# A two-layer RGCN with a GATv2 layer behind it: the RGCN layers staged a whole group apart, in half-group buffers

## The chip, the cores and the metric

The kernel runs on one core of a Trainium2 chip. The metric is the device time of one execution in microseconds, and for several executions their median. A core has five engines with a queue each: PE (TensorE, matmuls; its weight loads are listed apart as PEld), DVE (VectorE), ACT (ScalarE), POOL (GpSimd) and SP (SyncE, used here for DMA and for reading addresses). In this kernel POOL does little but issue the gathers.

## The reference

12,500 nodes with 128 features, 400,000 edges sorted by their target `dst`, 10 relations. The relation of an edge is the argmax of ten columns of its attributes.

```python
def _rgcn_layer(x, src, dst, edge_type, w_rel, root, bias):
    seg = dst * NUM_REL + edge_type
    sums = segment_sum(x[src], seg, num_segments=N * NUM_REL)
    cnt = segment_sum(ones(seg.shape), seg, num_segments=N * NUM_REL)
    mean = (sums / maximum(cnt, 1.0)[:, None]).reshape(N, NUM_REL, -1)
    return einsum('nrd,rdo->no', mean, w_rel) + x @ root + bias
...
h = relu(_layernorm(x))
h1 = relu(_rgcn_layer(h, src, dst, edge_type, w_rel1, root1, b1))
x = x + _rgcn_layer(h1, src, dst, edge_type, w_rel2, root2, b2)
h = relu(_layernorm(x))
# GATv2: 4 heads of 32, softmax over the edges of a target node
e = leaky_relu((h @ W_r)[dst] + (h @ W_l)[src], 0.2)
score = einsum('ehc,hc->eh', e, att)
x = x + segment_sum(softmax_by_dst(score) * (h @ W_l)[src], dst) + bias
```

## The kernel before

An RGCN layer is turned round: first every node's row is multiplied by all ten relation matrices, which makes a table of N x 10 rows in DRAM; then each edge fetches the row (source, relation), weighs it with 1/count, and the rows are summed by target node. `transform` makes the first table (98 tiles of 128 nodes: layer norm, transpose, three matmuls against `wall`, copies to SBUF, a DVE add of the bias, stores). `analyse` looks over the edges, and `sorted_edges` is the path that sorted edges take; the other path, `any_edges`, is not entered.

The 400,000 edges are 125 groups (G) of 128 x 25 (P x J): partition p holds 25 consecutive edges. Since targets are sorted, the nodes of a group lie in a window of 128 from a base node, and a sum by target is a matmul with a one-hot matrix. Three stages follow each other, each with a loop over the groups.

Layer 1 (`layer1`). `load` reads a group's attributes, finds the relation, makes the index `idx` (source x 10 + relation), issues 25 indirect DMAs on POOL (`gather`, L329; each fetches 128 rows of 512 bytes from the table) into one of three `xs` buffers, writes the wide one-hot `sb` in one DVE operation (L397) and counts edges by node and relation in 25 small matmuls (L401). `weights` completes the counts over the group's borders (three matmuls, L409 to L416), spreads them back to the edges through the one-hot `st` (L339, made in `by_node` from a broadcast of `drow_d`) in 25 matmuls (L422), and takes 1/count. `work` reads the base node (`base`: an ACT copy, L323, and a read on SP), and calls `sums`: 25 times a DVE one-hot scaled by the weight (`s`, L351, six buffers) and a matmul with it (L353), all into one PSUM tile. `carry` adds the border node's share from the group before (L359) and copies to SBUF (L362). Then come the own row, relu, a transpose (L128), three matmuls against `wall` (L445), ACT copies, and the stores of the second table. The loop calls `load(g)`, `weights(g-1)`, `work(g-2)`.

Layer 2 (`layer2`) gathers rows of the second table with the same `idx` and sums them with `sums` and `carry`; a layer norm, a transpose and one matmul make the tables of attention. Its loop calls `gather(g)` and `work(g-1)`.

Attention gathers rows of `h @ W_l` (132 wide), adds the target's row by matmuls (`pz`, L564 and L568), and makes scores (L571 to L574), maxima by scans, exponentials (`xw`, L626) and sums (L634). A group's `xw` is written after scores of the next two groups have been begun.

The framework sets each engine's order inside a stage by a planner with costs of its own, and adds the waits: a consumer waits for the notice (a semaphore count) of its producer, a writer of a buffer for the last reader of the buffer's older contents. In the program before, each matmul L353 waits for its one-hot and for its gather and gives a notice of its own.

## Time and profile before

| | |
|---|---|
| median of three runs | 15,672.79 us (15,643.28 to 15,676.48) |
| profiled execution, own time | 15,668.01 us |
| its span | 15,666.2 us |
| mean granted PE clock | 0.649 |
| busy share of the span | PE 47%, PEld 32%, DVE 38%, ACT 9%, POOL 62% |
| first gather of layer 1, of layer 2, of attention | 476.2, 5,650.7, 10,197.2 us |
| matmul instructions of L353 | 12,500 for 6,250 matmuls (two passes each) |

A row of the profile's groups names line, engine, operation, output and inputs, then its count, busy time and the mean in ns of one, and last how long the engine stood idle just before such instructions and what released it. "issue" as a releaser means that the profile shows nothing that the engine waited for; "remote" and "another core or an unknown queue" stand where no producer was found for the wait, though only one core runs. Idle time of an engine that is not the limit costs nothing, and so each stage has to be read by itself.

### The profile page before, as it was taken

The numbers are of one execution on the slowest core, as the hardware profiler recorded it, in microseconds if no ns is written. First come the engines' busy times: TensorE is split into PE (matmuls) and PEld (weight loads), VectorE is DVE, ScalarE is ACT, GpSimd is POOL, SyncE is SP. The second block draws the span as 40 slices with busy tenths as digits, with TensorE's granted clock in tenths as the row PEclk, the third lists the DMA queues.
The fourth block names the chain that finished last, engine by engine and source line by source line (L and its number), as shares of the span: only waits on it lengthen the run. The fifth ranks groups of instructions, "written<-read, shape, count | busy, mean of one in ns | idle before, by whom it ended". The sixth has DMA issues, their size and how long they took to land.

```text
span 15666.2 us, 128693 instructions
## 1 busy us (share of the span) xinstructions
PE 7415.8 (47%) x39724; PEld 5085.2 (32%) x39724; DVE 5907.1 (38%) x16500; ACT 1459.9 (9%) x4672; POOL 9747.0 (62%) x9384
## 2 busy tenths in 40 slices
PE   7344444444344433444344444445555555555555
PEld 2223333322232322333233333333333433333333
DVE  5333333333333322222222222244444544444444
ACT  2000000000000000000000000011111111111111
POOL 0566666666666656666666666656666666666665
PEclk9666666666666655555555555567766777767777
DMA  6322323323332211111111111122222222222221
GB/s 202 111 92 91 96 92 96 96 90 95 94 96 92 91 59 53 54 54 54 53 54 55 55 54 54 52 68 63 66 62 64 65 62 66 62 66 65 62 64 51
DMA packets 626065, 1164.38 MB, mean 74 GB/s; under 512 B 196480, under 2 KB 398830, under 8 KB 625390
## 3 DMA queue, kind: packets, MB, share of 16 engines
q0 software_dynamic: 300000, 621.40, 14.7%
q1 hardware_dynamic: 279544, 456.64, 8.8%
q10 hardware_dynamic: 45846, 78.02, 1.4%
q8 instruction: 341, 5.59, 0.1%
q14 instruction: 334, 2.74, 0.1%
HBM read 949.89 MB, written 205.49 MB: 74 GB/s over the span
## 4 chain that ended last, share of the span: by engine, by line
another core or an unknown queue 34%; POOL 19%; PE 19%; issue 14%; DVE 9%; DMA 4%; ACT 1%; ACTq 0%; SPq 0%; DVEq 0%; POOLq 0%
POOL xs L329 19%; PE ps L353 9%; DVE s L351 4%; PE pz L564 2%; PE pt L445 2%; DMA xs<-xl_d,src_i 2%; PE po L634 2%; DVE xw L626 1%; PE pz L568 1%; PE ps L150 1%; DMA xs<-t_d,idx 1%; DMA xt<-in_x_dram 1%; DVE sb L397 1%; PE ptr L128 1%
## 5 line engine op out<-in xcount | busy, mean ns | idle before, releaser
L329 POOL DMA_INDIRECT xs<-t_d,idx x6250 | 6310.8, 1010 | 3815.1 <-issue 2597.7
L353 PE MATMUL ps<-xs,s 128*128 128x128 f32 x12500 | 3119.0, 392 | 4870.9 <-issue 2743.4
L329 POOL DMA_INDIRECT xs<-xl_d,src_i x3125 | 3434.3, 1099 | 2014.9 <-DVE xw L626 1046.8
L353 PEld LDWEIGHTS ps<-xs,s 128*128 128x128 f32 x12500 | 2411.9, 267 | 5713.7 <-issue 3732.0
L351 DVE TENSOR_SCALAR s<-iota,dst_f,w 128x128 f32<-128x128 f32 x6250 | 2019.8, 359 | 5559.5 <-remote 3662.8
L564 PE MATMUL pz<-xs,ident 128*128 128x512 f32 x1750 | 1297.5, 834 | 2097.2 <-DMA xs<-xl_d,src_i 1219.8
L564 PEld LDWEIGHTS pz<-xs,ident 128*128 128x128 f32 x1750 | 355.6, 254 | 2229.6 <-issue 1559.7
L568 PEld LDWEIGHTS <-st 128*128 128x128 bf16 x9375 | 840.9, 126 | 622.7 <-issue 558.1
L572 DVE TENSOR_TENSOR lr<-lr,att 128x512 f32<-128x512 f32 x875 | 533.5, 624 | 1259.3 <-ACT lr L571 855.0
L568 PE MATMUL pz<-xr,st 128*128 128x128 bf16 x9375 | 956.5, 269 | 65.2 <-DVE st L339 49.9
L634 PE MATMUL po<-xw,s 128*128 128x132 f32 x6250 | 848.8, 297 | 76.5 <-DVE xw L626 41.2
L634 PEld LDWEIGHTS po<-xw,s 128*128 128x128 f32 x6250 | 815.9, 208 | 122.6 <-issue 64.4
L362 ACT COPY sm<-ps 128x128 f32<-128x128 f32 x250 | 66.3, 265 | 7564.5 <-PE ps L359 4030.8
L571 ACT ACTIVATE lr<-pz 128x512 f32<-128x512 f32 x875 | 476.8, 551 | 2776.4 <-remote 1425.1
L630 DVE TENSOR_TENSOR s<-iotab,dst_b 128x640 f32<-128x640 bf16 x625 | 506.6, 814 | 420.8 <-PE po L634 354.9
L626 DVE TENSOR_TENSOR xw<-xs,xw 128x640 f32<-128x640 f32 x625 | 484.0, 819 | 156.0 <-ACT xw L625 122.3
L574 DVE TENSOR_REDUCE sc<-lr 128x16 f32<-128x512 f32 x875 | 531.3, 620 | 1.0
L445 PE MATMUL pt<-wall,hT 128*128 128x512 f32 x750 | 504.3, 827 | 57.0 <-ACT hT L130 41.0
L397 DVE TENSOR_TENSOR sb<-iotab,dst_b 128x3200 bf16<-128x3200 bf16 x125 | 434.9, 3479 | 0.9 <-PE pcn L401 0.9
L424 DVE TENSOR_TENSOR cw<-pc,rh 128x250 f32<-128x250 f32 x125 | 51.9, 415 | 726.7 <-remote 619.8
L150 PE MATMUL ps<-wall,hT 128*128 128x512 f32 (+1 forms) x588 | 300.9, 647 | 29.1 <-DVE ts L155 21.4
L445 PEld LDWEIGHTS pt<-wall,hT 128*128 128x128 f32 x750 | 183.4, 268 | 305.1 <-issue 175.8
(187 smaller groups left out, 4532.6 us busy)
## 6 DMA issues: line engine op xcount, KB each, us to landing
db<-drow_d SPq DMA_DIRECT2D x250, 800.0 KB
xs<-t_d,idx POOLq DMA_INDIRECT x6250
t_d<-ts SPq DMA_DIRECT2D x125, 640.0 KB
m<-in_edge_attr_dram SPq DMA_DIRECT2D x125, 525.0 KB
t_d<-ts ACTq DMA_DIRECT2D x98, 640.0 KB
xs<-xl_d,src_i POOLq DMA_INDIRECT x3125
ac<-acc_d SPq DMA_DIRECT2D x250, 64.0 KB
xr_d<-xp SPq DMA_DIRECT2D x125, 96.0 KB
```

Source lines behind the costliest of these rows:

```text
L329: nc.gpsimd.indirect_dma_start(out=xs[:, j, :], out_offset=None, in_=table, in_offset=bass.IndirectOffsetOnAxis(ap=ids[:, j:j + 1], axis=0))
L351: nc.vector.tensor_scalar(s, iota, dst_f[:, g, j:j + 1], w[:, g, j:j + 1], op0=OP.is_equal, op1=OP.mult)
L353: nc.tensor.matmul(ps, s, xs[:, j, :], start=(j == 0), stop=(j == J - 1), skip_group_check=True)
L397: nc.vector.tensor_tensor(sb, iotab[:, None, :].to_broadcast([P, J, P]), dst_b[:, g, :, None].to_broadcast([P, J, P]), op=OP.is_equal)
L445: nc.tensor.matmul(pt[:, :n], hT, wall[:, c:c + n], start=True, stop=True)
L564: nc.tensor.matmul(pz[:, :n, :], ident, xs[:, j0:j0 + n, :D], start=True, stop=False, skip_group_check=True)
L568: nc.tensor.matmul(pz[:, j, :], st[:, j0 + j, :], xr[:, k, :], start=False, stop=(k == 2), skip_group_check=True)
L572: nc.vector.tensor_mul(lr[:, :n, :], lr[:, :n, :], att8[:, None, :].to_broadcast([P, n, P]))
L574: nc.vector.tensor_reduce(sc[:, :, j0:j0 + n].rearrange("p h j -> p j h"), lr[:, :n, :].rearrange("p j (h c) -> p j h c", h=H), AX.X, OP.add)
L626: nc.vector.tensor_mul(xw[:, :, :, :C], xs[:, j0:j0 + JW, :D].rearrange("p j (h c) -> p j h c", h=H), xw[:, :, :, C:].to_broadcast([P, JW, ...
L630: nc.vector.tensor_tensor(s, iotab[:, None, :].to_broadcast([P, JW, P]), dst_b[:, g, j0:j0 + JW, None].to_broadcast([P, JW, P]), op=OP.is_ ...
L634: nc.tensor.matmul(po, s[:, j, :], xw[:, j].rearrange("p h a -> p (h a)"), start=(j0 + j == 0), stop=(j0 + j == J - 1), skip_group_check=True)
```

## The change

- `first_table` takes the place of `transform` for the first table. The root matrix is multiplied the other way round, so that the own rows come out transposed (`accT_d`), with the bias in an ACT operation. (In `any_edges` they are transposed back; that path isn't taken.)
- Both RGCN layers run under a manual schedule: each engine takes instructions in the order of the text. Steps of one group lie a whole group apart. Attributes are loaded five groups ahead of the gathers, the index is made four ahead, the counts three.
- Gathers go into six half buffers of 13 and 12 rows; a half's one-hots are made in one of four buffers, a small matmul (into columns of PSUM that nobody reads) carries the waits of a half, and the half's 12 or 13 matmuls follow without waits and with one notice at the last.
- In layer 1 the gathered rows are the weights of those matmuls and the one-hots move, which gives the sums transposed: no transpose, no carry matmul and no `sm` copy there; `node` does the border on DVE. The own row enters the table by a matmul with `ident`.
- `sb` is written in 25 operations of 128 columns in place of one of 3,200.
- `base` reads the base node from `dst` in DRAM by a 4-byte DMA on SP in place of the ACT copy, in all three stages.
- Attention has four `xs` buffers in place of three and makes `dst_b` itself.

The diff, cut to its core: what comes, and of what goes only the lines that a new one stands against (the old functions are printed above).

```diff
+    def first_table():
...
+            for r in starts:
+                hT = load_x(xp, psum, r)
+                ts = xp.tile([P, R * D], F32, name="ts")
...
+                pa = psum.tile([P, P], F32, name="pa")
+                nc.tensor.matmul(pa, wall[:, R * D:], hT, start=True, stop=True)
+                at = xp.tile([P, P], F32, name="at")
+                nc.scalar.activation(at, pa, AF.Identity, bias=b1c)
+                nc.scalar.dma_start(tv[r:r + P, :], ts)
+                nc.sync.dma_start(accT_d[:, r:r + P], at)
...
             def base(cell, g):
-                nc.scalar.copy(cell, bi[0:1, g:g + 1])
+                nc.sync.dma_start(cell, dst[g * P * J:g * P * J + 1].rearrange("(o e) -> o e", o=1))
                 return nc.sync.value_load(cell, min_val=0, max_val=N - P if g < G - 1 else N)
...
+            def load_rows(pool, g):
+                db = pool.tile([P, J * P], BF16, name="db")
                 nc.sync.dma_start(db, drow_d[g:g + 1].rearrange("o j p -> o (j p)").to_broadcast([P, J * P]))
+                return db
+            def by_node(pool, db):
                 st = pool.tile([P, J, P], BF16, name="st")
                 nc.vector.tensor_scalar(st.rearrange("q j p -> q (j p)"), db, pcol, None, op0=OP.is_equal)
                 return st
...
+            HALVES = [(0, JH), (JH, J - JH)]
...
+                def gather_halves(pool, table, ids):
+                    xs = []
+                    for j0, n in HALVES:
+                        x = pool.tile([P, JH, D], F32, name="xs")
+                        for j in range(n):
+                            nc.gpsimd.indirect_dma_start(
+                                out=x[:, j, :], out_offset=None, in_=table,
+                                in_offset=bass.IndirectOffsetOnAxis(ap=ids[:, j0 + j:j0 + j + 1], axis=0))
+                        xs.append(x)
+                    return xs
+                def sums(sp, ps, g, xs, k, rows):
+                    j0, n = HALVES[k]
+                    s = sp.tile([P, JH, P], F32, name="s")
+                    for j in range(n):
+                        nc.vector.tensor_scalar(s[:, j, :], iota, dst_f[:, g, j0 + j:j0 + j + 1],
+                                                w[:, g, j0 + j:j0 + j + 1], op0=OP.is_equal, op1=OP.mult)
+                    nc.tensor.matmul(ps[:n, D:D + n], s[:, :n, 0], xs[k][:, :n, 0], start=(k == 0), stop=False,
+                                     skip_group_check=True)
+                    for j in range(n):
+                        a, b = (s, xs[k]) if rows else (xs[k], s)
+                        nc.tensor.matmul(ps[:, :D], a[:, j, :], b[:, j, :], start=(j0 + j == 0),
+                                         stop=(j0 + j == J - 1), skip_group_check=True)
...
+                        def load_attr(g):
+                            m = mp.tile([P, J, A], F32, name="m")
                             nc.sync.dma_start(m.rearrange("p j a -> p (j a)"), attrv[g])
+                            return m
+                        def prepare(g, m):
...
-                            eq = wp.tile([P, J, R], F32, name="eq")
-                            nc.vector.tensor_tensor(eq, z, mx[:, :, None].to_broadcast([P, J, R]), op=OP.is_equal)
-                            nc.vector.tensor_mul(eq, eq, rel_m)
+                            lt = wp.tile([P, J, R], F32, name="lt")
+                            nc.vector.tensor_tensor(lt, z, mx[:, :, None].to_broadcast([P, J, R]), op=OP.not_equal)
+                            nc.vector.scalar_tensor_tensor(lt, lt, float(R), iotar, op0=OP.mult, op1=OP.add)
                             rel = wp.tile([P, J], F32, name="rel")
-                            nc.vector.tensor_reduce(rel, eq, AX.X, OP.min)
-                            nc.vector.tensor_scalar_add(rel, rel, float(R))
+                            nc.vector.tensor_reduce(rel, lt, AX.X, OP.min)
                             nc.vector.scalar_tensor_tensor(idx[:, g, :], src_i[:, g, :], float(R), rel,
                                                            op0=OP.mult, op1=OP.add)
+                            rh = rp.tile([P, J, R], BF16, name="rh")
                             nc.vector.tensor_tensor(rh, iotar, rel[:, :, None].to_broadcast([P, J, R]), op=OP.is_equal)
+                            er = rp.tile([1, P], BF16, name="er")
+                            nc.vector.tensor_scalar(er, iota[0:1, :], eb[0:1, g:g + 1], None, op0=OP.is_equal)
                             sb = wp.tile([P, J, P], BF16, name="sb")
-                            nc.vector.tensor_tensor(sb, iotab[:, None, :].to_broadcast([P, J, P]),
-                                                    dst_b[:, g, :, None].to_broadcast([P, J, P]), op=OP.is_equal)
                             for j in range(J):
+                                nc.vector.tensor_scalar(sb[:, j, :], iotab, dst_f[:, g, j:j + 1], None, op0=OP.is_equal)
+                            return rh, er, sb
+                        def counts(g, rs, cs, own):
+                            pc = p1.tile([P, 2, R], F32, name="pcn")
+                            cn = cp.tile([P, 2, R], BF16, name="cn")
+                            if g < G:
+                                rh, _, sb = rs[g]
+                                for j in range(J):
+                                    nc.tensor.matmul(pc[:, 0, :], sb[:, j, :], rh[:, j, :], start=(j == 0),
+                                                     stop=(j == J - 1), skip_group_check=True)
+                            if own >= 0:
+                                pf = pc[:, 1, :]
+                                nc.tensor.matmul(pf, identb, cs[own][:, 0, :], start=True, stop=True,
                                                  skip_group_check=True)
-                            st = by_node(wp, wp, g)
+                                if own:
+                                    nc.tensor.matmul(pf[0:1, :], ecolb[:, own - 1:own], cs[own - 1][:, 0, :],
+                                                     start=False, stop=True, skip_group_check=True)
...
+                        def of_edges(db, cf):
+                            st = by_node(wp, db)
+                            pe = p1.tile([P, J, R], F32, name="pe")
                             for j in range(J):
+                                nc.tensor.matmul(pe[:, j, :], st[:, j, :], cf[:, 1, :], start=True, stop=True)
+                            return pe
...
+                        def load_node(g):
+                            at = cp.tile([P, P + 1], F32, name="at")
+                            b = base(at.bitcast(I32)[0:1, P:], g)
+                            nc.sync.dma_start(at[:, :P], accT_d[:, ds(b, P)])
...
+                        def node(g, ps, at, before):
+                            ha = cp.tile([P, P], F32, name="ha")
+                            nc.vector.tensor_add(ha, ps[:, :P], at[:, :P])
+                            if g:
+                                nc.vector.tensor_add(ha[:, 0:1], ha[:, 0:1], before)
+                            last = None
+                            if g < G - 1:
+                                jk = wp.tile([P, P], F32, name="jk")
+                                nc.vector.scalar_tensor_tensor(jk, iota, eb[:, g:g + 1], ps[:, :P],
+                                                               op0=OP.is_equal, op1=OP.mult)
+                                last = cp.tile([P, 1], F32, name="last")
+                                nc.vector.tensor_reduce(last, jk, AX.X, OP.add)
+                            hT = cp.tile([P, P], F32, name="hT")
+                            nc.scalar.activation(hT, ha, AF.Relu)
+                            return hT, last
+                        def table(g, hT, xb, b):
...
+                            for c in range(0, (R + 1) * D, 512):
                                 n = min(512, (R + 1) * D - c)
+                                pt = p3.tile([P, 512], F32, name="pt")
+                                nc.tensor.matmul(pt[:, :n], hT, wall[:, c:c + n], start=True, stop=(c + n <= R * D),
+                                                 skip_group_check=True)
+                                if c + n > R * D:
+                                    nc.tensor.matmul(pt[:, R * D - c:n], ident, xb, start=False, stop=True,
+                                                     skip_group_check=True)
+                                pts.append((c, n, pt))
+                            for c, n, pt in pts:
+                                nc.scalar.copy(ts[:, c:c + n], pt[:, :n])
...
+                        ms, rs, cs, pes, dbs, xs, pss, nodes, hTs = {}, {}, {}, {}, {}, {}, {}, {}, {}
+                        last = None
+                        ms[0] = load_attr(0)
+                        with tc.manual_schedule():
+                            for t in range(-4, G + 3):
+                                if 0 <= t < G:
+                                    xs[t] = gather_halves(xp, t1_d, idx[:, t, :])
+                                if 0 <= t + 5 < G:
+                                    ms[t + 5] = load_attr(t + 5)
+                                q = t - 2
+                                if 0 <= q < G:
+                                    nodes[q] = load_node(q)
+                                if 0 <= t + 3 < G or 0 <= t + 1 < G:
+                                    cs[t + 3] = counts(t + 3, rs, cs, t + 1)
+                                q = t - 1
+                                if 0 <= q < G:
+                                    weights(q, pes.pop(q), rs.pop(q)[0])
+                                    pss[q] = p2.tile([P, D + JH], F32, name="ps")
+                                    for k in range(2):
+                                        sums(sp, pss[q], q, xs[q], k, False)
+                                    xs.pop(q)
+                                q = t
+                                if 0 <= q < G:
+                                    pes[q] = of_edges(dbs.pop(q), cs[q + 2])
+                                q = t + 1
+                                if 0 <= q < G:
+                                    dbs[q] = load_rows(dp, q)
+                                q = t - 3
+                                if 0 <= q < G:
+                                    table(q, hTs.pop(q), *nodes.pop(q)[1:])
+                                q = t + 4
+                                if 0 <= q < G:
+                                    rs[q] = prepare(q, ms.pop(q))
+                                q = t - 2
+                                if 0 <= q < G:
+                                    hTs[q], last = node(q, pss.pop(q), nodes[q][0], last)
...
+                        xs, nodes, hns, hTs, pss, sms = {}, {}, {}, {}, {}, {}
+                        with tc.manual_schedule():
+                            for t in range(G + 4):
+                                if t < G:
+                                    xs[t] = gather_halves(xp, t2_d[:N * R, :], idx[:, t, :])
+                                q = t - 2
+                                if 0 <= q < G:
...
+                                    sms[q] = cp.tile([P, D], F32, name="sm")
+                                    nc.scalar.copy(sms[q], pss.pop(q)[:, :D])
+                                q = t - 1
+                                if 0 <= q < G:
+                                    ps = pss[q] = p2.tile([P, D + JH], F32, name="ps")
+                                    for k in range(2):
+                                        sums(sp, ps, q, xs[q], k, True)
+                                    xs.pop(q)
+                                    if q:
+                                        nc.tensor.matmul(ps[0:1, :D], ecol[:, q - 1:q], sms[q - 1],
+                                                         start=False, stop=True, skip_group_check=True)
+                                q = t - 2
+                                if 0 <= q < G:
...
-            with tc.tile_pool(name="gk", bufs=1) as kp, tc.tile_pool(name="gx", bufs=3) as xp, \
+            with tc.tile_pool(name="gk", bufs=1) as kp, tc.tile_pool(name="gx", bufs=4) as xp, \
...
-                    st = by_node(wp, wp, g)
+                    st = by_node(wp, load_rows(wp, g))
```

## The prediction, made before the changed kernel ran

> **What bounds the kernel now.** I read the page's busy shares first, then the groups, the windows by stage, the timeline of one group, and last the chain of waits. The profiled execution took 15,668.01 us for a span of 15,666.2; the median of the runs shown, 15,672.79, is 5 us above it. The start times of the gathers (POOL, L329) cut the span: preparation to 476, layer 1 to 5,650, layer 2 to 10,197, attention to the end. The windows of these stretches (columns: window, length, busy time of PE, PEld, DVE, ACT, POOL, then clock, DMA share, GB/s):
>
> ```profile
> 476.00:5650.00 5174.00, 2227.18 (x13945) 1527.41 (x13944) 1872.61 (x5105) 324.50 (x994) 3340.91 (x3125) 0.63 0.30 93
> 5650.00:10197.00 4547.00, 1844.52 (x6876) 1363.22 (x6876) 1205.52 (x4130) 286.88 (x1004) 2969.91 (x3125) 0.57 0.19 54
> 10197.00:15666.00 5469.00, 3009.00 (x18123) 2061.70 (x18123) 2561.71 (x6377) 737.47 (x2372) 3434.30 (x3125) 0.71 0.23 63
> ```
>
> No engine is full anywhere. POOL is nearest, and its row hides a second cost: inside a group a gather takes 0.94 us and the next begins 0.30 later, so one costs 1.249 us and 25 cost 31.2. That is 3,903 us per stage of 125 groups, the floor of all three. Above it layer 1 has 1,271 us, layer 2 has 644, attention 1,566. The pauses between gathers say where: in layer 1, 828 us in pauses over 4.6 us and 353 in about 140 gathers that took some 4 us instead of 0.94; in layer 2, 560 us in 119 pauses; in attention 1,009 in 103 long pauses and 434 in short ones. The rest is 47 us between the layers, 40 before attention, 60 at the end, and small change. The groups (busy, mean ns, idle before and its releaser):
>
> ```profile
> L353 PE MATMUL ps<-xs,s 128*128 128x128 f32 x12500 | 3119.0, 392 | 4870.9 <-issue 2743.4
> L329 POOL DMA_INDIRECT xs<-xl_d,src_i x3125 | 3434.3, 1099 | 2014.9 <-DVE xw L626 1046.8
> L351 DVE TENSOR_SCALAR s<-iota,dst_f,w 128x128 f32<-128x128 f32 x6250 | 2019.8, 359 | 5559.5 <-remote 3662.8
> L362 ACT COPY sm<-ps 128x128 f32<-128x128 f32 x250 | 66.3, 265 | 7564.5 <-PE ps L359 4030.8
> ```
>
> DVE waits 5,560 us to write one-hots of 0.36 us, mostly on something "remote", and ACT waits on PE for sums that cost PE little. The timeline of DVE in one group of layer 1, and POOL's at its end, show what that is:
>
> ```profile
> 3029.91 0.35 DVE L351 TENSOR_SCALAR s<-iota,dst_f,w 128x128 f32<-128x128 f32 x1 [3.21 <-remote]
> 3034.14 0.34 DVE L351 TENSOR_SCALAR s<-iota,dst_f,w 128x128 f32<-128x128 f32 x1 [3.89 <-remote]
> 3039.06 0.35 DVE L351 TENSOR_SCALAR s<-iota,dst_f,w 128x128 f32<-128x128 f32 x1 [4.57 <-remote]
> 3044.66 0.38 DVE L351 TENSOR_SCALAR s<-iota,dst_f,w 128x128 f32<-128x128 f32 x1 [5.25 <-remote]
> 3050.27 0.35 DVE L351 TENSOR_SCALAR s<-iota,dst_f,w 128x128 f32<-128x128 f32 x1 [5.23 <-remote]
> ...
> 3059.89 1.11 DVE L351 TENSOR_SCALAR s<-iota,dst_f,w 128x128 f32<-128x128 f32 x4
> ...
> 3061.24 3.48 DVE L397 TENSOR_TENSOR sb<-iotab,dst_b 128x3200 bf16<-128x3200 bf16 x1
> ```
> ```profile
> 3049.05 0.94 POOL L329 DMA_INDIRECT xs<-t_d,idx  x1 [0.30 <-issue]
> 3060.38 0.94 POOL L329 DMA_INDIRECT xs<-t_d,idx  x1 [10.39 <-issue]
> 3061.63 3.91 POOL L329 DMA_INDIRECT xs<-t_d,idx  x1 [0.31 <-issue]
> ```
>
> s has 6 buffers, so the one at 3050.27 waits for the matmul six before it, which had ended at 3024.7 (PE's timeline). Its rows had landed earlier still: PE was on group 60, gathered by 2868. So what arrives late is the word that a matmul is done. As POOL gathers on without a break the steps grow to 3.2, 3.9, ... 5.25 us and stop growing near 5.6; a few us after POOL pauses at 3050 everything pending arrives at once and the s follow at 0.27 us. Matched over all groups, the wait of an s is 0.4 us when the gather stream is 4 to 8 us old, 1.3 at 8 to 16, 2.4 at 16 to 20, 3.6 at 24 to 28, 5.1 (median) beyond 40. It counts notices, not matmuls: the 25 count matmuls of L401, which give one, were also heard of some 27 us late. POOL in turn pauses because its 3 buffers come free only when that chain of 25 notices is through (or because idx, behind the s in DVE's order, is late), and the pause releases the chain. Nobody else is late: DVE's and ACT's notices take 0.03 us. Hence the odd chain of waits:
>
> ```profile
> another core or an unknown queue 34%; POOL 19%; PE 19%; issue 14%; DVE 9%; DMA 4%; ACT 1%; ACTq 0%; SPq 0%; DVEq 0%; POOLq 0%
> ```
>
> **The change, part by part.**
>
> *One notice a half (both layers).* In the program before, layer 1 has about 35 notices of PE a group, layer 2 about 28. After it layer 1 has 8 (counts, two halves of the sums, the edges' counts, four in the table), layer 2 has 5 (two halves, carry, transpose, table). [...] At 5.6 us each, in an endless stream, 8 notices need 45 us against a floor of 31.2, so layer 1 still falls behind slowly; 5 need 28, so layer 2 does not. A fresh stream is faster: by the waits above it passes some 18 notices in its first 31 us, then 5.6 a group. With three groups of buffers between POOL and the sums, demand 8(n-2.5) passes supply 12.4+5.6n near n=13. Each such pause costs the 6 to 7 us seen in layer 2 (7.3 at 7422). I take one each ten groups, 0.7 us a group in layer 1 and next to nothing in layer 2.
>
> *A whole stage between steps, idx four groups ahead.* This takes idx and the carry off POOL's path. What is late next is the loop weights, s, sums, edges' counts, weights: 25 one-hots at 0.36 (9 us), st 1.05, PE about 1, ACT and weights 2, with half of the rest of DVE's work (DVE 15 us a group by the window) fitting beside it. About 15 us without late notices, 31 with three at 5.6: just hidden.
>
> *sb as 25 pieces (L397 before).* The 3.48 us op costs POOL 3.0 each time, 353 us. Nearest rows for the pieces: st (bf16, one source, 1.05 us at 605.41) stretched the gather beside it from 0.94 to 1.48; the f32 one-hots of 0.27 us add 0.02 to 0.03. [...] I take 0.65 us a group, 81 in all. st stays at 0.54, 68.
>
> *PE, DVE, ACT in the layers.* Transposed sums drop the transpose, the sm copy and the carry matmul of layer 1; node adds two to four DVE ops of 0.3 us. PE (2,227 us in 5,174) and DVE (1,873) have room, so I count nothing; were the floor gone, DVE's 15 us a group would be next.
>
> *base on SP.* ACT loses 375 copies of 0.19 us; SP gains as many 4-byte transfers and waits for each[...]. Behind it are at/ac, xb, db, the stores, and in attention xr, pen and db. In the layers these are wanted a stage later: nothing. [...] I take 0 because gathers run ahead of PE there.
>
> *First table.* DVE loses 98 adds of 281 ns (27 us), ACT gains 98 bias copies, PE 98 weight loads of 0.2, SP 98 stores ahead of its loads. Between -27 and +40: first gather at 480 instead of 476.
>
> *Attention: a fourth xs buffer.* Today gather g+3 begins 0.3 us (median) after the last xw (L626) of group g, which comes 128 us after g's first gather. Four buffers at an unchanged 128 would be 32 us a group, all of it gained. But PE still has about 24 notices a group there. When two groups ran unbroken (12,065 to 12,134) PE's pz stood still from 12,109 to 12,139, then did the whole next group in 10 us. A 31 us stream passes some 15 to 18 of 24, the others need a pause of 8 to 10: 40 to 42 a group; two groups unbroken pass 21 of 48 and pause 27: 45. Against 43.75 I take 43, so -100.
>
> Sum: start 480; layer 1 3,903 + 68 + 81 + 90 + 20 of small change + 65 for three steps after the last gather = 4,227; layer 2 3,903 + 44 + 10 + 55 = 4,012; attention 5,469 - 100 = 5,369. Together 14,088, and with the 5 us to the median and outside the span some 14,095.
>
> **The rivals.**
>
> *Attention takes the whole buffer (0.22).* If the order of work leaves PE notices in each pause, 36 to 38 us a group: attention 4,600, total 13,330. For it: DVE xw 1,046.8 as POOL's releaser. Against it: the standstill at 12,109.
>
> *The layers still pause every group (0.20).* The notices may bunch so that POOL waits once a group, or each second: 6 us (3) in layer 1, 4.5 (2.5) in layer 2, attention unchanged. Total 15,340 (14,790). For it: layer 2 does so now with 28 notices. Against it: 5 to 8 are fewer than a stream passes.
>
> *Pauses too short to release anything (0.08, slower).* Deeper buffers could leave POOL running until the last notice it needs, at 5.6 us each. Then layer 1 takes 8 x 5.6 = 45 us a group (5,670), and attention, with longer streams, 48 (6,000). With layer 2 at 4,012 that is 16,160. It decides from the point where the periods of layer 1 and attention add up to over 89.5 us (now 85.2, and 4.3 that layer 2 gives back). Against it: in the first 100 us of layer 1, unbroken, the spacing saturated, and ended with the first pause.
>
> *It doesn't do what it says:* if late notices come from waiting on gathered rows and not from their number, the halves change little; that is the second rival's time.
>
> **How the numbers follow.** The forecast has 0.50 and a range of its own of 13,850 to 14,500 (attention 41.5 to 44.5 a group, pauses in layer 1 of 0 to 2 us). Reaching to both neighbours, 13,250 to 15,000, leaves out the slow rival and the end of the second. 0.2%, 31 us, is about what can be told from no change: 0.90 faster, 0.02 same, 0.08 slower.
>
> **What would show it.** Right: in both layers POOL's gathers 1.25 to 1.28 us apart with pauses under 1 us a group on average; no gathers near 4 us; layer 2 near 32 us a group, layer 1 near 33.5; the s in bursts of 12 or 13; the waits of ACT's and DVE's consumers on PE still several us long, but harmless. Attention near 43 with xw still the releaser. Wrong: regular pauses of 5 us or more in layer 2, gathers beside sb of over 1.2 us, a first gather after 520, or attention under 40.

## The result: 0.9% faster where 10% was forecast

The changed kernel takes 15,524.36 us (median of five runs, 15,480.84 to 15,558.41) against 15,672.79 us of the kernel before: 0.9907 of its time, 95% interval 0.9883 to 0.9931. The forecast of 14,095 was far off, and the range of 13,250 to 15,000 did not hold it. By stages of the profiled execution (15,522.6 us of span), from first gather to first gather:

| us | before | forecast | after |
|---|---|---|---|
| start of layer 1 | 479 | 480 | 433 |
| layer 1 | 5,172 | 4,227 | 5,020 |
| layer 2 | 4,547 | 4,012 | 4,510 |
| attention to the end | 5,469 | 5,369 | 5,560 |

(479 is where the first gather itself starts; the prediction's 476 was the record of its wait.) The start gained 46 us, layer 1 151, layer 2 37, and attention lost 91. A ratio is the thing to compare below: from chip to chip the kernel before itself differed by 1% (15,507 to 15,689 us). The changed kernel's own ratio came out at 0.9907 and, on another chip (e9), at 0.9934, so half a percent between chips says little. "Period" is a stage from its first to its last gather in the profiled run, divided by 125 groups: 41.0, 36.1 and 43.3 us before, 39.7, 35.7 and 43.9 after.

The windows of the three stages of after (columns as in the prediction):

```profile
433.00:5453.00 5020.00, 1901.20 (x14372) 1570.08 (x14372) 2085.34 (x8241) 255.48 (x627) 3039.95 (x3126) 0.63 0.30 96
5453.00:9963.00 4510.00, 1587.57 (x7375) 1266.05 (x7375) 1053.89 (x4133) 250.92 (x877) 2981.86 (x3126) 0.59 0.19 54
9963.00:15522.00 5559.00, 2676.79 (x18123) 1899.41 (x18123) 2561.89 (x6379) 712.65 (x2125) 3399.05 (x3125) 0.70 0.22 62
```

POOL's busy time in layer 1 fell from 3,341 to 3,040 us: the gathers of some 4 us are gone. Yet the stage became only 151 us shorter, because the pauses remain. From the groups of the page, and from those of DVE in layer 2 (the last line):

```profile
L385 POOL DMA_INDIRECT xs<-t_d,idx x6250 | 6021.7, 963 | 3481.6 <-issue 1774.0
L403 PE MATMUL ps<-xs,s 128*128 128x128 f32 x6250 | 1291.9, 352 | 1773.5 <-issue 1772.6
L396 DVE TENSOR_SCALAR s<-iota,dst_f,w 128x128 f32<-128x128 f32 x6250 | 1633.7, 364 | 14.5 <-issue 8.4
...
L619 DVE TENSOR_TENSOR rest<-ts,xp 128x128 f32<-128x128 f32 x124 | 36.2, 292 | 3186.7 <-ACT xp L616 2347.9 <-ACT hT L134 812.1 <-ACT ts L610 26.6
```

The one-hots (now L396) wait for nothing any more, 14.5 us where it was 5,559.5: that much the half buffers did. But the same wait has moved. In layer 2 DVE now stands at `rest` (L619) for 3,187 us, 25 us a group, behind an ACT that waits for PE. And PE's matmuls of the sums, which have no wait and no notice of their own, stood idle for 1,773 us on "issue", on nothing that the profile shows. The timeline of PE and DVE late in a stream of gathers (layer 1) shows that idle time one by one:

```profile
3045.18 0.37 PE L403 MATMUL ps<-s,xs 128*128 128x128 f32 x1 [2.44 <-issue]
3047.97 0.37 PE L403 MATMUL ps<-s,xs 128*128 128x128 f32 x1 [2.42 <-issue]
3050.77 0.37 PE L403 MATMUL ps<-s,xs 128*128 128x128 f32 x1 [2.43 <-issue]
...
3046.58 0.28 PEld L403 LDWEIGHTS ps<-s,xs 128*128 128x128 f32 x1 [1.82 <-issue]
3049.37 0.29 PEld L403 LDWEIGHTS ps<-s,xs 128*128 128x128 f32 x1 [2.50 <-issue]
...
3047.98 0.42 DVE L433 TENSOR_TENSOR lt<-m,mx 128x250 f32<-128x250 f32 x1 [7.64 <-issue]
3049.38 0.42 DVE L434 SCALAR_TENSOR_TENSOR lt<-lt,iotar 128x250 f32<-128x250 f32 x1 [0.98 <-DVE lt L433]
3050.78 0.41 DVE L436 TENSOR_REDUCE rel<-lt 128x25 f32<-128x250 f32 x1 [0.98 <-DVE lt L434]
```

Every instruction shown is late, notice or not: weight load, matmul, weight load follow each other at 1.40 us, DVE's operations too; most of SP's instructions, in the same stretch of the trace, take 0.69 to 0.71 us and start some 0.70 or 1.40 us apart. In the last 9 us of all the streams that a pause ends, 77% of the steps from one weight load or matmul to the next are 1.35 to 1.45 us long in layer 1, and 65% in layer 2. An f32 matmul is four such instructions, hence the 5.6 us that the prediction took for the price of a notice. And POOL's pauses in layer 2, once a group, with PE as releaser:

```profile
7377.91 0.94 POOL L385 DMA_INDIRECT xs<-t_d,idx  x1 [4.47 <-PE ps L642]
7413.60 0.94 POOL L385 DMA_INDIRECT xs<-t_d,idx  x1 [4.47 <-PE ps L642]
7449.37 0.94 POOL L385 DMA_INDIRECT xs<-t_d,idx  x1 [4.51 <-PE ptr L132]
```

The half that the last of these gathers overwrites had been summed 23 us earlier: half 0 of group 53 of layer 2 ended at 7,426.7, the gather that may replace it began at 7,449.4. From then until 7,449.1 the trace records no update of PE's semaphore at all, and so it is in 98 of 100 groups looked at (22.9 us, median). PE's notices are late indeed, as the prediction had it, and this one came only in the pause. In layer 1 there are 121 such pauses of 8.0 us (970 us), in layer 2 121 of 4.3 us (523 us). The chain of waits:

```profile
issue 33%; PE 26%; another core or an unknown queue 23%; DVE 10%; POOL 5%; DMA 2%; ACT 1%; ACTq 0%; SPq 0%; DVEq 0%; POOLq 0%
```

### The profile page after: what moved, and what is told of

Read it like the earlier page. It is cut to its first block, busy times and chain, and to the rows that moved or that the text cites. A ratio compares the mean times of both kernels' runs of the same rounds, so it can differ in the third digit from the quotient of the medians.

```text
span 15522.6 us, 129908 instructions
## 1 busy us (share of the span) xinstructions
PE 6481.7 (42%) x40797; PEld 4891.6 (32%) x40797; DVE 5936.8 (38%) x19524; ACT 1355.3 (9%) x4022; POOL 9423.0 (61%) x9384
## 4 chain that ended last, share of the span: by engine, by line
issue 33%; PE 26%; another core or an unknown queue 23%; DVE 10%; POOL 5%; DMA 2%; ACT 1%; ACTq 0%; SPq 0%; DVEq 0%; POOLq 0%
PE ps L403 11%; PE pz L695 4%; PE pz L699 3%; POOL xs L385 3%; DVE s L396 2%; POOL xs L356 2%; PE po L765 2%; DVE sb L445 2%; PE pt L608 1%; PE ps L280 1%; DVE s L761 1%; DMA xs<-t_d,idx 1%; DVE xw L757 1%; DVE st L369 1%
## 5 line engine op out<-in xcount | busy, mean ns | idle before, releaser
L385 POOL DMA_INDIRECT xs<-t_d,idx x6250 | 6021.7, 963 | 3481.6 <-issue 1774.0
L356 POOL DMA_INDIRECT xs<-xl_d,src_i x3125 | 3399.4, 1088 | 2139.3 <-DVE xw L757 1128.1
L695 PE MATMUL pz<-xs,ident 128*128 128x512 f32 x1750 | 1115.8, 730 | 2377.6 <-ACT lr L702 1387.7
L403 PE MATMUL ps<-xs,s 128*128 128x128 f32 x6250 | 1291.9, 352 | 1773.5 <-issue 1772.6
L403 PE MATMUL ps<-s,xs 128*128 128x128 f32 x6250 | 1221.8, 348 | 1690.9 <-issue 1690.9
L403 PEld LDWEIGHTS ps<-s,xs 128*128 128x128 f32 x6250 | 1118.7, 260 | 1858.3 <-issue 1853.9
L403 PEld LDWEIGHTS ps<-xs,s 128*128 128x128 f32 x6250 | 1129.8, 260 | 1785.0 <-issue 1775.9
L396 DVE TENSOR_SCALAR s<-iota,dst_f,w 128x128 f32<-128x128 f32 x6250 | 1633.7, 364 | 14.5 <-issue 8.4
L619 DVE TENSOR_TENSOR rest<-ts,xp 128x128 f32<-128x128 f32 x125 | 36.5, 292 | 3186.7 <-ACT xp L616 2347.9
L699 PEld LDWEIGHTS <-st 128*128 128x128 bf16 x9375 | 768.4, 118 | 618.3 <-issue 488.6
L445 DVE TENSOR_SCALAR sb<-iotab,dst_f 128x128 bf16<-128x128 bf16 x3125 | 591.2, 253 | 526.6 <-issue 525.4
L399 PE MATMUL ps<-xs,s 128*13 128x13 f32 x1000 | 130.0, 189 | 1257.4 <-issue 1182.6
```

The costliest lines, as they stand in the source:

```text
L356: nc.gpsimd.indirect_dma_start(out=xs[:, j, :], out_offset=None, in_=table, in_offset=bass.IndirectOffsetOnAxis(ap=ids[:, j:j + 1], axis=0))
L385: nc.gpsimd.indirect_dma_start(out=x[:, j, :], out_offset=None, in_=table, in_offset=bass.IndirectOffsetOnAxis(ap=ids[:, j0 + j:j0 + j + 1 ...
L396: nc.vector.tensor_scalar(s[:, j, :], iota, dst_f[:, g, j0 + j:j0 + j + 1], w[:, g, j0 + j:j0 + j + 1], op0=OP.is_equal, op1=OP.mult)
L403: nc.tensor.matmul(ps[:, :D], a[:, j, :], b[:, j, :], start=(j0 + j == 0), stop=(j0 + j == J - 1), skip_group_check=True)
L445: nc.vector.tensor_scalar(sb[:, j, :], iotab, dst_f[:, g, j:j + 1], None, op0=OP.is_equal)
L695: nc.tensor.matmul(pz[:, :n, :], ident, xs[:, j0:j0 + n, :D], start=True, stop=False, skip_group_check=True)
```

## The experiments

The theories: N, the prediction's, that PE's notices are late and each has a price; I, that every instruction start is slow while gathers stream; later B, that each gather leaves a backlog behind which slows the other engines, and W, its opposite, that a slower pace of the gathers only adds its own time. L and D are two accounts of layer 2's pauses, told with e11. All runs below are compared with the kernel before on the same chip. The expectations of the first eight took 15,520 us for the changed kernel; on their two chips the kernel before ran 15,513 and 15,507, so the changed one would stand there near 15,370 (0.9907), and their differences are to be read from that.

### Half the matmuls, more of them, and a notice for each

```diff
-                    for j in range(n):
+                    for j in range(0, n, 2):      # e1: sums
...
-                                         stop=(j0 + j == J - 1), skip_group_check=True)
+                                         stop=(j0 + j + 2 >= J), skip_group_check=True)
```

> Theory N (the prediction's: PE's notices are late, and each costs up to 5.6 us): notices are as many as in the changed kernel, so the layers keep their periods of 39.7 and 35.7 us a group: 15,520 us within 60. Theory I (under an unbroken gather stream every instruction of PE, DVE, ACT and SP is slow to start, whether or not it waits or notifies, about 1.4 us for one of PE): 12 of 25 matmuls less, of four PE instructions each, is 48 less of about 120 in layer 2 and of about 230 in layer 1. Layer 2 loses its pauses (31.5 us a group, -520), layer 1 about half of its own (-500): 14,500 us. (Every second matmul of a half's sums is left out.)

Ratio 0.9600 (0.9584 to 0.9616), some 480 us less than the changed kernel. Layer 1's period fell to 36.1 us, as theory I has it; layer 2's stayed at 35.3, against theory I. Its pauses became fewer (90) and longer (5.4 us), with a sum of 482 us for 523.

```diff
+                        nc.tensor.matmul(ps[0:1, D + JH:], identb[:, 0:1], identb[:, 0:1], start=True,
+                                         stop=True, skip_group_check=True)      # e3: behind each matmul
...
```

> Behind each of the 25 matmuls of a group's sums a 1x1 bf16 matmul that nobody reads, without wait or notice: two PE instructions of 0.1 us each. Theory N: 5 us of PE time a group that is free, 15,520 us within 80. Theory I: 50 instructions a group more than a stream lets through, the rest must go in POOL's pause: 5 to 10 us a group in both layers, 16,700 us (16,200 to 17,500).

Ratio 1.0759 (1.0722 to 1.0796). (The sums come out different here; the cause was not shown.) Layer 1 went to 49.5 us a group. POOL's gathers of layer 1 beside those of e1, in the timeline, only those after a pause; first e3, then e1:

```profile
3009.08 0.94 POOL L385 DMA_INDIRECT xs<-t_d,idx  x1 [20.29 <-PE ps L403]
3059.53 0.94 POOL L385 DMA_INDIRECT xs<-t_d,idx  x1 [19.56 <-PE ps L403]
```
```profile
3039.67 0.95 POOL L385 DMA_INDIRECT xs<-t_d,idx  x1 [4.04 <-PE ps L403]
3075.90 0.95 POOL L385 DMA_INDIRECT xs<-t_d,idx  x1 [4.40 <-PE ps L403]
```

The pause of layer 1 grows with PE's work: 4 us in e1, 8 in the changed kernel, 19 in e3. Layer 2 stayed at 35.7 even here, so something else holds layer 2. But e3 doesn't show that the number of instructions is what counts in layer 1. The small matmuls took more of PE's own time than the 0.1 us that I had given them. PE's sums once they run close together, first in e3, then in the changed kernel:

```profile
3050.26 0.80 PE L403 MATMUL ps<-s,xs 128*128 128x128 f32 x2
3050.99 0.16 PE L405 MATMUL ps<-identb 128*1 128x1 bf16 x1
3051.08 0.80 PE L403 MATMUL ps<-s,xs 128*128 128x128 f32 x2
```
```profile
3055.67 4.44 PE L403 MATMUL ps<-s,xs 128*128 128x128 f32 x20 [1.73 <-issue]
```

A matmul with its small one takes 0.82 us, one alone 0.44 us (ten in 4.44): for 25 of them 9.5 us more, which is all that the period grew by. (PE's granted clock was lower there, too: 0.50 in the 17 us from 3,045 of e3, 0.74 in the 20 us from 3,050 of the changed kernel.) In layer 1 the rest of PE's work has to be done in the pause; whether the number of its instructions or their time sets the length is not separated by e1 and e3.

```diff
-                    s = sp.tile([P, JH, P], F32, name="s")
                     for j in range(n):
+                        s = sp.tile([P, P], F32, name="s")      # e2: 52 of them
...
-                    nc.tensor.matmul(ps[:n, D:D + n], s[:, :n, 0], xs[k][:, :n, 0], start=(k == 0), stop=False,
-                                     skip_group_check=True)
...
```

> Each one-hot in a tile of its own again (52 of them, as much room as the four halves), each matmul with its own wait and its own notice, no counted matmul. Theory N: 25 notices a group for 2 undo what the halves were for, 15,700 us or more. Theory I: the same matmul instructions, so the same time: 15,520 us within 80.

Ratio 0.9817 (0.9774 to 0.9860), not slower than the changed kernel but, if anything, faster (e4, on the same chip, has 0.9890): 23 notices more and eight PE instructions fewer a group (the counted matmul, f32, is four). A notice has no price of 5.6 us, and theory N is out: layer 2 took 35.4 us a group here, 35.5 in e4.

### What the pauses of layer 2 are not

```diff
+                            nc.gpsimd.memset(pace, 0.0)      # e4: 128x1, behind each gather
```

> A POOL memset of 128x1 behind each gather of the layers (some 0.1 to 0.2 us each). If nothing but POOL's own time counts, 25 x 250 x 0.15 us = 900 us more: 16,400 us. If it is the density of the gather stream that slows the other engines, the pauses shrink by as much as the gathers take more: layer 2 the same, layer 1 a few us a group less: 15,000 to 15,500 us.

Ratio 0.9890 (0.9850 to 0.9931), the changed kernel's within the intervals. Inconclusive, since it paced nothing: the memset of 0.14 us lay in the 0.30 us between two gathers, which still came each 1.249 us.

```diff
-                    with tc.tile_pool(name="hk", bufs=1) as kp, tc.tile_pool(name="hx", bufs=6) as xp, \
+                    with tc.tile_pool(name="hk", bufs=1) as kp, tc.tile_pool(name="hx", bufs=12) as xp, \
```

> Layer 2 with twelve half buffers for six (six groups in place of three). If POOL pauses there because the buffers are too few for the lateness of a notice: pauses go, 31.5 us a group, 15,000 us. Theory I (what PE may start or announce in a stream is limited, the rest needs a pause): fewer and longer pauses, 35 to 36 us a group as now, 15,510 us within 80.

Ratio 0.9893 (0.9876 to 0.9909); layer 2 at 35.4 us a group, a pause of 4 us in nearly each. Twice the buffers do nothing: PE is only further behind, its sums of a half ending 174 us (median) after that half's last gather, where it was 69 us.

```diff
-                                out=x[:, j, :], out_offset=None, in_=table,
+                                out=x[:, j, :D // 2], out_offset=None,      # e8
+                                in_=table.rearrange("n (h d) -> (n h) d", h=2),
...
```

> The gathers of both layers fetch 64 columns (256 bytes a row) in place of 128, as many rows and instructions as before; the other half of the buffers is zero. If the bytes of the gathers slow the other engines: shorter lateness, layer 1 near 36 us and layer 2 near 33 us a group, 14,800 us. If it is their number or their issue on POOL: 15,510 us within 80.

Ratio 1.0212 (1.0194 to 1.0229): layer 1 at 39.0 us as its neighbours on that chip (39.1), layer 2 at 39.8, slower. In layer 1 it isn't the bytes. Why layer 2 alone is worse is open: the edit also puts six fixed tiles in place of the pool's buffers, and a gather there begins some 4 us before the sums of the half that it overwrites have ended, so its waits are others as well.

```diff
-                                    hTs[q] = relu_T(cp, p2, hns.pop(q))      # e11: relu a stage after the transpose,
...
+                                q = t - 6                                    # table's copies a stage after its matmul
+                                if 0 <= q < G:
+                                    table(q, pts.pop(q), nodes.pop(q)[1])
```

> Layer 2 with the relu of the transposed rows and the second half of the table one stage later, so that no step waits for a matmul of its own stage. Theory L (POOL's pause of 4.2 us a group stands because ACT, then DVE's rest and the next one-hots, wait for a PE notice of the same stage, which comes only in a pause): the pause goes, layer 2 near 32 us a group, 15,080 us. Theory D (a pause is needed anyway to let through what PE has to start): fewer and longer pauses, 34.5 to 37 us a group, 15,510 us within 150.

Ratio 0.9892 (0.9876 to 0.9909). The waits of DVE at `rest` went from 3,125 us (in the copy of the changed kernel below) to 22, and the period stayed at 35.69 us in both. Theory L as it was put, a notice of the same stage, falls. But DVE did not become free of PE's notices. It now stands as long at `x` (L599), behind ACT's copy of the sums, which waits for PE (147 us in the copy):

```profile
L599 DVE TENSOR_TENSOR x<-sm,ac 128x128 f32<-128x128 f32 x122 | 35.7, 293 | 3262.8 <-ACT sm L637 3144.4 <-issue 118.4
```

> The same with every second matmul of the sums left out in both layers (48 of about 118 PE instructions a group of layer 2). In the changed kernel's order that alone left layer 2 at 35.3 us a group. Theory L: 32 us, as without it. Theory D: only now do two groups pass in one pause: 33 to 34 us a group, where the run with all matmuls stays above 34.5. Layer 1 as in the first run with half the matmuls, 36 us: 14,700 us.

Here e1's edit stands on top of e11's. Ratio 0.9625 (0.9592 to 0.9659), layer 2 at 35.3 us, outside what either theory expected. It is the telling run. POOL now pauses after every second group, 62 times, for twice as long:

```profile
7454.89 0.95 POOL L385 DMA_INDIRECT xs<-t_d,idx  x1 [8.16 <-remote]
7525.80 0.95 POOL L385 DMA_INDIRECT xs<-t_d,idx  x1 [8.46 <-remote]
```

62 pauses of 7.7 us add up to 483 us; the changed kernel's 121 to 523. In layer 2 of these runs a pause is in proportion to the stream before it, 0.12 to 0.14 us per us, with all matmuls or half of them, with six half buffers or twelve. PE's instructions show it without any wait: six of them within 1.2 us are first seen again 3.5 us (median) after the end of the stream's last gather in the changed kernel, and 7.1 us after it in e12, where the stream is twice as long. I read that as a price of the gathers, an estimated 0.15 to 0.17 us each on top of 1.249 (7.7 us over 50 gathers in e12, 4.3 over 25 in the changed kernel). Two places don't follow the proportion: layer 2 of e8 (8.8 us after some 31) and attention (19 us after some two groups), which have waits of their own. The data themselves are not late: in the trace's DMA packets the last piece of a gather lands 2.1 to 2.2 us (median) after its issue, at the start of a stream and after 60 us of it.

### Pacing the gathers

```diff
                                 in_offset=bass.IndirectOffsetOnAxis(ap=ids[:, j0 + j:j0 + j + 1], axis=0))
+                            for _ in range(2):                   # e13, e15; e14: range(j % 2 * 2)
+                                nc.gpsimd.memset(zero[:, :P], 0.0)
```

> The two memsets behind every second gather only: on average 1.37 to 1.42 us a gather. Theory W: half of what the run before adds, +1,100 us. Theory B: the backlog grows little or not at all: layer 2 as it is (35.5 us), layer 1 37 and attention 40: ratio 0.96, between 0.94 and 0.98.

("The run before" is e13, below.) Ratio 0.9703 (0.9671 to 0.9735). Gathers come each 1.25 and 1.59 us in turn, and in both layers not one pause over 4.6 us is left (121 in layer 1 of the changed kernel): layer 1 at 37.4 us a group, layer 2 at 36.2, which is the pace itself, 1.45 us a gather on average. DVE's wait at `rest` is as long as ever there (3,266 us in layer 2), and harmless. PE's sums no longer trickle. The same stretch of layer 2 as above, on PE: the small matmul, then 26 instructions of a half in 5.3 us, within the stream:

```profile
7438.93 0.21 PE L403 MATMUL ps<-xs,s 128*13 128x13 f32 x2 [13.46 <-DMA xs<-t_d,idx]
7439.07 5.32 PE L407 MATMUL ps<-xs,s 128*128 128x128 f32 x26
```

What it waits for is a gather (13.46 us): the sums have caught up with the data, where they were two groups behind. Steps of 1.3 to 1.5 us from one matmul instruction of PE to the next fell from 894 (copy of the changed kernel) to 24 in the whole trace. The chain of waits is POOL's at last:

```profile
POOL 54%; issue 16%; another core or an unknown queue 13%; PE 11%; DVE 3%; DMA 1%; ACT 1%; ACTq 0%; POOLq 0%; SPq 0%; DVEq 0%
```

> Two POOL memsets of 128x128 behind each gather, in all three stages (the earlier single memset of 128x1 disappeared in the 0.30 us between gathers): an estimated 1.5 to 1.6 us a gather. Theory W: 0.3 us x 9,375 = 2,300 us more than the changed kernel. Theory B: no backlog at this pace, so no late notices and no pauses but the pace itself: layer 2 38 us a group (+2), layer 1 38 to 39 (-1), attention 39 to 41 (-3): the ratio to the kernel before near 0.98, between 0.95 and 1.00.

Ratio 1.0590 (1.0560 to 1.0621), above what theory B had said: each gather 1.59 us, no pauses either, layer 1 at 42.7 and layer 2 at 41.4. Past e14's pace a slower one buys nothing and costs itself; a pace between 1.25 and 1.45 us was not tried in the layers of the changed kernel. In attention the planner had put memsets elsewhere (some of them behind the end): the gathers stayed at 1.25 us in e14 and came each 1.34 in e13, and attention kept its pauses in both, at 43.4 and 43.3 us a group.

> The kernel before with the two memsets behind each gather. Theory W: +2,300 us, ratio 1.15. Theory B: the same notices are no longer late here either: the layers near 39 us a group and attention 39 to 41, ratio 0.97 to 1.00.

The two memsets in the `gather` of the kernel before. Ratio 1.1000 (1.0967 to 1.1033), and it says little: the planner left some 1,600 us of memsets behind the last gather, and the gathers' pace became 1.334 us. Even so layer 1's period fell from 41.0 to 39.2 us; layer 2's rose to 37.4, with 55 pauses over 4.6 us left.

```diff
+                    for _ in range(j % 2 * 2):                   # e17, in attention's gather
+                        nc.gpsimd.memset(xs[:, j, :], 0.0)
```

> The layers as in the run with memsets behind every second gather; in attention two memsets of every second row of xs ahead of the gather that overwrites it, so that the pace holds there too, about 1.45 us a gather. Theory B: notices are prompt in attention as well, and its 43.4 us a group fall to 37 to 40: ratio 0.93 to 0.95. If attention is held by something else, the pace only adds to it: 0.97 to 1.00.

Ratio 0.9449 (0.9427 to 0.9471), the best version here: 14,832 us where the kernel before took 15,689. Tied to the rows that the gather overwrites, the memsets stay in place; attention falls from 43.4 to 40.8 us a group, its pauses over 4.6 us from 955 us (e14) to 337. Less than the 37 to 40 expected: attention keeps waits of its own. Its chain:

```profile
POOL 61%; issue 18%; another core or an unknown queue 8%; PE 7%; DVE 4%; DMA 1%; ACT 1%; ACTq 0%; POOLq 0%; SPq 0%; DVEq 0%
```

> The same pace in the layers only, no memsets in attention, three xs buffers there. The layers at 37.4 and 36.2 us a group as before; attention 42.5 to 43.5: ratio 0.965 to 0.975.

The pace of e14 without attention's memsets, with e5's three buffers. Ratio 0.9652 (0.9627 to 0.9677): layers as in e14, attention unpaced at 43.2. The pace in attention is thus worth some 2% of the kernel (with it goes a fourth buffer, which by e5 is worth nothing).

### sb, the fourth buffer, and a copy

```diff
-                            for j in range(J):      # e6
-                                nc.vector.tensor_scalar(sb[:, j, :], iotab, dst_f[:, g, j:j + 1], None, op0=OP.is_equal)
+                            nc.vector.tensor_tensor(sb, iotab[:, None, :].to_broadcast([P, J, P]),
+                                                    dst_b[:, g, :, None].to_broadcast([P, J, P]), op=OP.is_equal)
```

> The wide one-hot sb in one DVE operation of 3.48 us again. The prediction's sum (POOL bounds layer 1, the operation holds one gather for 3 us, the 25 pieces 0.65): +2.4 us a group, 15,800 us. Theory I (layer 1 is bound by how fast instructions start while the gathers run; POOL has 8 us of pause a group to spare): the stall is hidden in the pause, and 24 DVE instructions a group are saved: 15,450 us within 60.

Ratio 0.9760 (0.9744 to 0.9776): taking the split back made the kernel 1.5% faster. POOL's stalls did come back, as its timeline shows (a pause, then two stalls):

```profile
3045.55 0.94 POOL L387 DMA_INDIRECT xs<-t_d,idx  x1 [10.36 <-PE ps L405]
...
3069.07 3.29 POOL L387 DMA_INDIRECT xs<-t_d,idx  x1 [0.31 <-issue]
...
3104.73 4.24 POOL L387 DMA_INDIRECT xs<-t_d,idx  x1 [0.30 <-issue]
```

But layer 1's period fell to 37.9 us (39.1 in its neighbours on that chip): a stall of POOL may serve as a pause too, and DVE has 24 instructions fewer; which of the two it is was not separated.

> sb in one operation and three xs buffers in attention, with the two memsets behind each gather. Under theory B what these two gave (DVE instructions that need not start in a stream) is worth nothing more once instructions start at once: the ratio of the run with the two memsets, plus up to 1% for the 3 us stall of sb. Under theory W: 0.976 and the added POOL time, 1.12.

The edits of e6 and e5 with e13's pace. Ratio 1.0734 (1.0703 to 1.0765). Where the pace leaves no pauses to hide in, the stall of sb costs its full length: layer 1 at 45.2 us against 42.7 in e13, 2.6 us a group. So the split is right once POOL is the bound, as at e13's pace, and wrong before.

```diff
-            with tc.tile_pool(name="gk", bufs=1) as kp, tc.tile_pool(name="gx", bufs=4) as xp, \
+            with tc.tile_pool(name="gk", bufs=1) as kp, tc.tile_pool(name="gx", bufs=3) as xp, \
```

> Attention with three xs buffers again, all else as changed. The same attention instructions in the same order ran 5,294 to 5,484 us between first and last gather in four kernels that differ only in the layers; before, with three buffers, 5,409. If the fourth buffer is worth little: 15,510 us within 100. If it is the fourth buffer that cost the changed kernel 75 us there: 15,430 or less. The prediction's gain of 100 would give 15,610.

Ratio 0.9836 (0.9819 to 0.9852), on the same chip as e7 (0.9893): three buffers are no worse than four. Attention itself took 42.6 us a group here and 42.7 in e7; the 0.6% lie between layer 2's last gather and attention's first, 56 us here and 100 in e7 with its twelve buffers. The fourth is worth nothing.

> The changed kernel itself, word for word. Its twins with something immaterial altered (a POOL memset behind each gather; more buffers in layer 2; three buffers in attention) ran 150 to 250 us faster, in stages that they do not touch. If that is luck of the single program, this one takes 15,510 us within 40; if it lies in how the two sides of a comparison are run, 15,300.

Ratio 0.9934 (0.9917 to 0.9952), 15,553 us where the kernel before took 15,670. The premise of this expectation was mistaken: the twins had run on chips where the kernel before is 1% faster too, so there was no luck to explain. Its interval overlaps that of the result.

> Three steps back at once: sb in one operation, own tiles and notices for the one-hots without the counted matmul, three buffers in attention. Theory I counts instructions: 24 fewer on DVE and 8 fewer on PE a group in layer 1, each worth 0.05 to 0.15 us a group: layer 1 near 37 us, layer 2 as it is: 15,000 us within 100. The prediction's account (sb holds POOL, notices are dear) says 15,700 or more.

The edits of e2, e6 and e5 together. Ratio 0.9753 (0.9737 to 0.9769), layer 1 at 38.5 us, attention 43.3. The 15,282 us miss the 15,000 expected, which had counted from the wrong chip; by ratio it is e6 over again, and the three steps don't add up.

## Why the prediction was wrong

- **The floor.** "One costs 1.249 us and 25 cost 31.2 ... the floor of all three" is the step that failed most. The pauses above it were taken for waits that a better pipeline removes, and the sum put those of layer 2 at next to nothing. They measured 523 us, all of layer 2's miss of 498. Every unpaced variant of the changed kernel but the one that fetches half the bytes took 35.3 to 35.7 us a group there, whatever was done to buffers, matmuls and order, and it took 36.2 with the gathers spread out and no pause at all. So the pauses are the other part of the gathers' price there, as far as these runs go.
- **"It counts notices, not matmuls."** Wrong: 23 notices more a group cost nothing (e2). PE's notices are late, but so are most of PE's instructions late in a stream (steps of 1.40 us); the count matmuls of L401, heard of 27 us late as one notice, are themselves 50 instructions. The change replaced 25 notices by two but left the matmuls; PE's matmul instructions rose from 39,724 to 40,797. In layer 1 this is the rest of the miss: PE's work that a stream holds up goes into the pause, 8.0 us a group where the sum had 0.7, and the period is 39.7 us against the 35.4 or so of layer 2. Half the matmuls took 3 to 4 us off it (e1).
- **The loop "just hidden".** In layer 2 DVE did wait 25 us a group for a notice of its own stage, as feared. e11 moved this wait without removing it, so it doesn't show what it costs; e14 has the same wait and not one pause, so the wait alone makes none.
- **sb.** The mechanism was right: the pieces hold POOL almost nothing (121 gathers of over 1.2 us in layer 1, 68 us too long in all, which is what the sum had for st alone; it had 81 more for the pieces). The gain of 353 us was not there to be had, since POOL's stall lay in its pauses (e6).
- **Attention.** -100 was forecast, +91 came. The fourth buffer did not help (e5), and it may be the loss: on one chip attention took 43.25 us a group with three (e10) and 43.7 with four (e9), on another 42.6 and 42.7 (e5, e7). "Two groups unbroken" is what the fourth allows, and POOL's waits for xw rose from 1,046.8 to 1,128.1 us:

```profile
L356 POOL DMA_INDIRECT xs<-xl_d,src_i x3125 | 3399.4, 1088 | 2139.3 <-DVE xw L757 1128.1
```

- **The start** was better than its bounds of -27 to +40: -46 us. This was read from the traces only, and no run does the new first table alone.
- **The rival** "the layers still pause every group" named what happened, 6 and 4.5 us against 8.0 and 4.3 measured, and its 15,340 lies 1.2% from the result (its own terms add up to some 15,370 to 15,410). That the total came so near is in part luck, since the 91 us that attention lost are not in it. It was given 0.20 on the argument that 5 to 8 notices are fewer than a stream passes, the same mistaken count. A layer 2 that paused 4.5 us a group with 28 notices and whose releaser was PE could have been asked: would half as many change it? The trace had the answer in the "issue" time of PE's matmuls, 2,743 us before.

What stays open is what the backlog consists of. In the stretch shown PE, DVE and SP start in steps of 0.70 us or twice that, while POOL's gathers keep their 1.249 us and the rows land 2.1 to 2.2 us after issue; no run shows the cause.

## What to carry to other kernels

Before a pause is called a wait, see whether it grows with what went before it: a pause in proportion to the stream that precedes it may be part of the stream's price, which buffers and order did not remove here. When instructions without any wait start at even steps on several engines at once, don't look for the wait that holds them, and try spreading the traffic that coincides with it: two small operations behind every second gather, in all three stages, took 4.6% off the changed kernel, five times what the restructuring itself had brought. A stall removed from an engine that has pauses to spare is worth nothing until the pauses are gone, as sb shows both ways.

## What the runs showed of the hardware

- Late in a stream of gathers (one per 1.249 us, 128 rows of 512 bytes), at 3,045 to 3,052 us of the changed kernel, PE and DVE instructions without waits start 1.40 us apart, SP's some 0.70 or 1.40 us; in the last 9 us of the streams 77% (layer 1) and 65% (layer 2) of PE's steps are 1.35 to 1.45 us. In layer 2, after a stream of 31 us, PE's first run of six instructions within 1.2 us comes some 3.5 us after the end of its last gather, after 62 us some 7 (e12).
- PE's notices were late by more than 20 us: in layer 2 of the changed kernel none is recorded for 22.9 us (median) after the end of a group's first half.
- With gathers 1.25 and 1.59 us apart in turn (e14, 1.45 on average in layer 2) steps of 1.3 to 1.5 us between PE's matmul instructions fell from 894 to 24, and the 26 instructions of the half shown start 0.2 us apart within the stream. At 1.34 us attention kept its pauses (e13).
- In the changed kernel's layers the gathered rows land 2.1 to 2.2 us (median) after issue, at the start of a stream and late in it. With 256 bytes a row in place of 512 layer 1 took 39.0 us a group, its neighbours on that chip 39.1 (e8).
- A POOL memset of 128x1, 0.14 us, left the gathers 1.249 us apart (e4); two of 128x128 took a gather to 1.59 us (e13).
- A small bf16 matmul between f32 ones of 128x128 took a step of the sums from 0.44 to 0.82 us, at a granted clock of 0.50 in place of 0.74 (e3).
